# Layer 0's attention: its other products four at a time behind one of four steps, and gelus in threes

## The chip, the cores and the metric

The kernel runs on one core of a Trainium2 chip. Its time is the device time of one execution in microseconds; the median of three runs is given. The engines are TensorE (matmuls, with its weight loads apart), VectorE, ScalarE, GpSimd and SyncE, which issues most DMAs. A profile of one execution records when each instruction ran.

## The reference, cut to what matters

Four layers work on eight images of 384 channels and 32 x 32 pixels. The change lies in layer 0, and in it in the attention part:

```python
q = _dwproj(x, dw_q, g_q, b_q, pw_q).reshape(B, heads, hd, N)   # depthwise conv, batch norm, exact gelu, then pw
k = _dwproj(x, dw_k, g_k, b_k, pw_k).reshape(B, heads, hd, N)
v = _dwproj(x, dw_v, g_v, b_v, pw_v).reshape(B, heads, hd, N)
attn = jax.nn.softmax(jnp.einsum('bhcn,bhcm->bhnm', q, k) * scale, axis=-1)
out = jnp.einsum('bhnm,bhcm->bhcn', attn, v).reshape(B, C, H, W)
out = jnp.einsum('oc,bchw->bohw', w_out, out)
return _bn(out, g_out, b_out)
```

There are B = 8 images, 8 heads of 48 channels and N = 1024 pixels. Everything is in float32. The batch norm after the attention needs the moments of all images.

## The kernel before, in words

Layer 0 first runs the depthwise convolutions of all images and stores them (`raw`). Then comes the attention, which is the stretch from about 415 to 1845 us of the profile. An image's three tensors are loaded as `g` (`load_b`), and each gets its batch norm and gelu in place, in three chunks of 128 x 1024 (`gelu_chunk`, L483, on ScalarE). The gelus of image b + 1 are done during image b, at steps that the table `GELUS` names.

The heads are handled in four pairs. Three pairs hold the first channels of two heads each, the fourth is gathered by small DMAs (`gather_last`, L460) from the rows left over. An image has 32 **steps**: four pairs, times two halves of the query pixels (`h`), times four steps of two key blocks of 128 (`kc` = 0, 2, 4, 6; NS = 2). I number an image's steps 0 to 31. Four steps of one pair and half make a unit. The loop over steps does this:

- It issues the scores of the **next** step (`scores`, L623): eight matmuls a step, each in a tile of 64 rows by 64 columns of the array with 512 columns streamed, into two PSUM buffers `s` of two banks each. (The profile records each of the kernel's float32 matmuls as two, so a step's scores show as x16 and a product as x6.) ScalarE takes their exponential (L630), which gives `p`.
- If `GELUS` names this step, the gelus of the next image's chunks stand here on ScalarE, behind those exponentials.
- It weighs the values with this step's `p` (`weigh`, L638): again eight matmuls of 64 x 64 tiles, into two PSUM banks `pav` that are held for the whole unit.
- In some steps it takes other products from a queue, `todo`, and issues them. At the end of a unit VectorE normalises (`normalise`, L595 to L609): it reads the two `pav` banks, transposes, takes the reciprocal and writes `att`. For the fourth pair `place_last` (L471) copies the rows into `att` by twelve DMAs.

The other products use the whole 128 x 128 array. Each is one PSUM bank from the pool `bank` of four, which `pav` shares:

- `project` (L558): 3 matmuls by 512 columns give half of q or of k for one pair. The copy out alternates between ScalarE (first half) and VectorE (second half), through `evac` (L76, L78). After the second half, two small gathers go to SyncE's queue.
- `values` (L531): 3 matmuls by 384 columns give a block of 128 pixels of v, copied by VectorE (L538).
- `out_project` (L575): 3 matmuls by 512 columns of the output projection. It loads a piece `xh` of x (L572) and stores its result `ot` (L588), both by SyncE's queue, with two buffers each; VectorE copies, takes moments and forms two sums (L584, L587, L477, L478). In the last image ScalarE does the copy and issues the store.

An image queues, in this order: 4 projections at step 0, 6 output products of the image before at step 4, 4 projections at step 8, 8 values of the next image at step 16, and 4 projections of the next image at step 24. The first image's own values are also in the queue at the start, and the last image queues 3 of its own output products at step 28. ScalarE's order is the order of the program (`manual_schedule`); the other engines' orders are made by the framework's scheduler, which keeps each product group where the loop puts it on TensorE.

Of the kernel before, what the change touches and what calls it, by code (L numbers as in the profile page):

```python
# [15 lines left out]
KC = C // P  # L16
# [36 lines left out]
def tile_kernel(ctx: ExitStack, tc: tile.TileContext, i: dict, out: bass.AP):  # L53
# [10 lines left out]
    def big(name):  # L64
        return ps_big.tile([P, N], F32, tag="big", name=name)

    def bank(name):
        return ps_mm.tile([P, HALF], F32, tag="mm", name=name)
# [144 lines left out]
    def load_b(b):  # L213
        acts[b] = {}
        for v in (0, 1, 2) if b == 0 else (2, 1, 0):
            acts[b][v] = image(f"g{v}_{b}")
            load_image(acts[b][v], raw[v][b])

    with ExitStack() as pa:
# [120 lines left out]
        sts, taps, todo, later, normed = {}, [], {}, list(work), {0}  # L340
# [141 lines left out]
    def gelu_chunk(g, v, c):  # L482
        nc.scalar.activation(  # L483
            g[:, c, :], g[:, c, :], AF.Gelu,
            bias=ss0[:, v, 1, c : c + 1], scale=ss0[:, v, 0, c : c + 1],
        )
# [5 lines left out]
    with ExitStack() as pb:  # L492
# [10 lines left out]
        def values_tile(s):  # L503
            t = wb.tile([P, NT8, 2 * NH0, 32], F32, name=f"vt{s}")
            nc.gpsimd.memset(t, 0.0)
            nc.gpsimd.memset(t[:, :, :, HQ0 : HQ0 + 1], 1.0)
            vts.append(t)

        values_tile(0)
        for v, nm in enumerate(("wq0", "wk0", "wv0")):  # L510
# [9 lines left out]

        GELUS = {
            s: [divmod(i, KC) for i in range(2 * k, min(2 * k + 2, 3 * KC))]
            for k, s in enumerate((7, 9, 11, 13, 17))
        }

        def values(b, t):
            pv = bank(f"pv{b}_{t}")
            for c in range(KC):  # L530
                nc.tensor.matmul(  # L531
                    pv[:, :C],
                    lhsT=acts[b][2][:, c, t * P : (t + 1) * P],
                    rhs=w_in[2][:, c, :],
                    start=(c == 0),
                    stop=(c == KC - 1),
                )
            nc.vector.tensor_copy(  # L538
                vts[b % 2][:, t, :, :HQ0],
                pv[:, :C].rearrange("p (h d) -> p h d", d=HQ0),  # L540
            )

        def fetch(k):

            b, t = divmod(k, 2)
            fetched[b, t] = image(f"f{b}_{t}")
            load_image(fetched[b, t], o_dram[b] if t else x_img[b])

        def project(b, pr, v, h):
            if h == 0:  # L550
                qks[b, pr, v] = qp.tile([P, N], F32, tag=f"qk{v}", name=f"qk{v}_{b}_{pr}")
                if pr == 0:
                    qks[b, KC, v] = qp.tile(
                        [P, N], F32, tag=f"ql{v}", name=f"ql{v}_{b}", bufs=1
                    )
            pq = bank(f"pq{v}_{b}_{pr}_{h}")
            for c in range(KC):
                nc.tensor.matmul(  # L558
                    pq,
                    lhsT=w_in[v][:, c, pr * P : (pr + 1) * P],  # L560
                    rhs=acts[b][v][:, c, h * HALF : (h + 1) * HALF],
                    start=(c == 0),
                    stop=(c == KC - 1),
                )
            evac(qks[b, pr, v][:, h * HALF : (h + 1) * HALF], pq)
            if h == 1:
                gather_last(qks[b, KC, v], qks[b, pr, v], pr)

        def out_project(b, m, h):
            hs = slice(h * HALF, (h + 1) * HALF)  # L570
            xh = op.tile([P, HALF], F32, tag="xh", name=f"xh{b}_{m}_{h}")
            nc.sync.dma_start(out=xh, in_=x_img[b][:, m, hs])  # L572
            po = bank(f"po{b}_{m}_{h}")
            for c in range(KC):
                nc.tensor.matmul(  # L575
                    po,
                    lhsT=wo0[:, c, m * P : (m + 1) * P],
                    rhs=atts[b][:, c, hs],
                    start=(c == 0),
                    stop=(c == KC - 1),  # L580
                )
            ot = op.tile([P, HALF], F32, tag="ot", name=f"ot{b}_{m}_{h}")
            if b + 1 < B:
                nc.vector.tensor_copy(ot, po)  # L584
            else:
                nc.scalar.copy(ot, po)
            nc.vector.bn_stats(ost[:, m, 2 * b + h, :], ot)  # L587
            (nc.sync if b + 1 < B else nc.scalar).dma_start(out=o_dram[b, :, m, hs], in_=ot)  # L588
            cross(b, m, h, xh, ot)
# [43 lines left out]
        def weigh(b, pr, kc, pav, p):  # L633
            for k in range(2):
                r = slice(64 * k, 64 * k + 64)
                for j in range(2):
                    hd = 2 * pr + j
                    nc.tensor.matmul(  # L638
                        pav[k][64 * j : 64 * j + 64, :],
                        lhsT=vts[b % 2][r, kc, 2 * hd : 2 * hd + 2, :].rearrange(  # L640
                            "p a b -> p (a b)"
                        ),
                        rhs=p[r, j * HALF : (j + 1) * HALF],
                        start=(kc == 0),
                        stop=(kc == NT8 - 1),
                    )
# [8 lines left out]
        NS = 2  # L655
# [5 lines left out]
        todo = [lambda t=t: values(0, t) for t in range(NT8)]  # L661
        todo.pop(0)()

        def scores_of(b, pr, h, kc):
            return [scores(b, pr, h, kc + k) for k in range(NS)]
# [4 lines left out]
        for n, (b, pr, h, kc) in enumerate(steps):  # L670
            if kc == 0:
                if pr == 0 and h == 0:
                    atts[b] = ap_.tile([P, KC, N], F32, tag="att", name=f"att{b}")
                    if b + 1 < B:
                        load_b(b + 1)
                    else:
                        for k in range(3):
                            fetch(k)
                if b == 0 and pr == 1 and h == 0:
                    values_tile(1)  # L680
                if b + 1 == B and pr == 2 and h == 0:
                    for k in range(3, 5):
                        fetch(k)
                if b + 1 == B and pr == 3 and h == 1:
                    todo += [lambda m=m: out_project(B - 1, m, 0) for m in range(KC)]
                if h == 0 and pr + 1 < KC:
                    todo += [
                        lambda v=v, q=q, b=b, pr=pr: project(b, pr + 1, v, q)
                        for v in (1, 0) for q in range(2)
                    ]  # L690
                if pr == 0 and h == 1 and b > 0:
                    todo += [
                        lambda m=m, q=q, b=b: out_project(b - 1, m, q)
                        for m in range(KC) for q in range(2)
                    ]
                if pr == 2 and h == 0 and b + 1 < B:
                    todo += [lambda t=t, b=b: values(b + 1, t) for t in range(NT8)]
                if pr == 3 and h == 0 and b + 1 < B:
                    todo += [
                        lambda v=v, q=q, b=b: project(b + 1, 0, v, q)  # L700
                        for v in (1, 0) for q in range(2)
                    ]
                pav = [bank(f"pav{b}_{pr}_{h}_{k}") for k in range(2)]
            cur = nxt
            if n + 1 < len(steps):
                nxt = scores_of(*steps[n + 1])
            if b + 1 < B:
                for v, c in GELUS.get(n % (len(steps) // B), ()):
                    gelu_chunk(acts[b + 1][2 - v], 2 - v, c)
            for k in range(NS):  # L710
                weigh(b, pr, kc + k, pav, cur[k])

            if n % NS or (b == 0 and pr == 0 and h == 0):
                for _ in range(min(2, len(todo))):
                    todo.pop(0)()
            if kc == NT8 - NS:
                normalise(b, pr, h, pav)
# [19 lines left out]
    _, sco, sho = sc_o  # L737
# [51 lines left out]
    with tc.If(redo > 0):  # L789
        with ExitStack() as pb:  # L790
# [13 lines left out]
            with tc.For_i(0, B) as bi:  # L804
# [40 lines left out]
                for pr in range(NPAIR0):  # L845
                    qt, kt = qks[0][:, pr, :], qks[1][:, pr, :]
                    for h in range(2):
                        pav = bank(f"pav_e{pr}_{h}")
                        for j, r in enumerate(HR):
                            hd = 2 * pr + j  # L850
                            pt = qp.tile([P, NT8, HALF], F32, tag="pt", name=f"pt_e{pr}_{h}_{j}")
                            for qc in range(4):
                                q0 = h * HALF + qc * P
                                nm = f"_e{pr}_{h}_{j}_{qc}"
                                s = big(f"s{nm}")
# [13 lines left out]
                                for kg in range(2):  # L869
                                    tp = bank(f"tp{nm}_{kg}").rearrange("p (k q) -> p k q", k=4)  # L870
                                    for k in range(4):
                                        kc = kg * 4 + k
# [952 lines left out]
```

## Time and profile before

| what | value |
| --- | --- |
| three runs, us | 3834.8, 3829.8, 3833.54; median 3833.54 |
| the profiled execution's own time, us | 3834.06 |
| its span, first to last instruction, us | 3832.2 |
| mean granted TensorE clock | 0.975 |
| TensorE busy over the span, us | 3646.2 (95%) |
| period of one image of attention (first gelu to first gelu, images 3 and 4), us | 1179.34 - 1001.95 = 177.39 |
| exponentials of layer 0 (L630), us | 512 of 1.02 |
| gelus from L483 | 72 of 1.23 |
| loads of the gelu table (L483) and of the exponential's (L630) | 36 and 36, 1.28 each |

A line of a timeline gives the start in us from the span's start, the length in us, the engine, the line of the kernel, the operation, what it writes and reads, how many neighbouring instructions are merged into the line, and in brackets how long the engine stood idle ahead of it and who released it. PE is TensorE, PEld its weight loads, DVE VectorE, ACT ScalarE, POOL GpSimd, SP SyncE. Matmul ends are modelled, so distances between starts say more than lengths.

### The profile page before, as it was taken

To read this page: it belongs to the slowest core of one execution; us is meant where nothing else is said; L and a number is where in the kernel's file an instruction comes from. 1 tells how busy PE (TensorE), PEld (TensorE's weight loads), DVE (VectorE), ACT (ScalarE), POOL (GpSimd) and SP (SyncE) were. 2 spreads that over 40 slices of the span, in tenths; PEclk is the share of its full clock that TensorE was granted. 3 is DMA by queue.
4 is the path that set the end of the run, shared out by engine and by line. 5 is a ranking of instruction groups with operands and counts; after the bars stand their busy time and mean duration, and the time that the engine had idled before them with its cause. 6 is when DMAs were issued, how large, how long until landed. Compare 5 with 4: busy or idle time off the path is not lost.

```text
span 3832.2 us, 39353 instructions
## 1 busy us (share of the span) xinstructions
PE 3646.2 (95%) x15754; PEld 1520.9 (40%) x15754; DVE 1823.4 (48%) x2826; ACT 1314.7 (34%) x1557; POOL 235.5 (6%) x170
## 2 busy tenths in 40 slices
PE   7999899999999999999899999999999999999748
PEld 3444333333333333333344445444444444445213
DVE  5876223232323232332256665475656646565544
ACT  2222454554546353534112323223232222313102
POOL 0000000000000000000000100101011010100321
PEclk9999999999999999999899999999999999999868
DMA  6777211121202121111620000101001010010000
GB/s 200 245 235 241 100 53 43 53 61 40 74 24 72 27 69 38 59 49 50 233 81 33 17 33 19 48 17 33 33 17 34 17 50 17 25 42 1 17 17 18
DMA packets 83097, 242.64 MB, mean 63 GB/s; under 512 B 18336, under 2 KB 18864, under 8 KB 82520
## 3 DMA queue, kind: packets, MB, share of 16 engines
q1 hardware_dynamic: 69894, 200.56, 15.7%
q10 hardware_dynamic: 13008, 39.43, 3.0%
q8 instruction: 128, 2.10, 0.2%
q14 instruction: 67, 0.55, 0.0%
HBM read 122.78 MB, written 75.50 MB: 52 GB/s over the span
## 4 chain that ended last, share of the span: by engine, by line
PE 39%; DVE 9%; POOL 1%; issue 1%; ACT 1%; DVEq 0%; ACTq 0%; POOLq 0%
PE y L1251 10%; PE ph L1232 8%; DVE y L1320 5%; PE pq L1367 3%; PE pw L1341 3%; PE s L1504 3%; PE pf L1609 3%; PE pav L1520 2%; PE pss L1546 1%; DVE hd L1218 1%; DVE off L1415 1%; PE pk L1478 1%; PE xsb L1464 1%; PE pv L1487 1%; POOL tap L1323 1%
## 5 line engine op out<-in xcount | busy, mean ns | idle before, releaser
L630 ACT ACTIVATE p<-s 128x1024 f32<-128x1024 f32 x512 | 496.4, 1021 | 497.1 <-PE s L623 496.8
L1251 PE MATMUL y<-hd,w_sb 128*128 128x512 f32 x1080 | 493.4, 601 | 3.6 <-DVE hd L1218 3.6
L638 PE MATMUL pav<-p,vt 64*64 64x512 f32 x4096 | 486.4, 589 | 0.0
L1232 PE MATMUL ph<-h,w_sb 128*128 128x512 f32 x1104 | 483.6, 594 | 0.0
L623 PE MATMUL s<-qk,qk 48*64 48x512 f32 x3072 | 373.1, 600 | 4.4 <-ACT p L630 4.4
L381 PE MATMUL pk<-st,cw_sb 126*126 126x512 f32 x720 | 321.5, 608 | 3.6 <-DVE ga_a L118 3.3
L1232 PEld LDWEIGHTS ph<-h,w_sb 128*128 128x128 f32 x1104 | 207.8, 190 | 252.5 <-issue 249.4
L1251 PEld LDWEIGHTS y<-hd,w_sb 128*128 128x128 f32 x1080 | 198.8, 191 | 250.4 <-issue 236.3
L638 PEld LDWEIGHTS pav<-p,vt 64*64 64x64 f32 x4096 | 156.2, 133 | 285.3 <-issue 285.0
L595 DVE COPY ta<-pav 128x512 f32<-128x512 f32 x64 | 44.3, 692 | 439.1 <-PE pav L638 436.1
L1320 DVE SCALAR_TENSOR_TENSOR y<-h,tap,y 128x961 f32<-128x961 f32 (+1 forms) x184 | 233.5, 1295 | 1.6
L381 PEld LDWEIGHTS pk<-st,cw_sb 126*126 126x126 f32 x720 | 140.1, 197 | 177.7 <-issue 170.7
L1415 DVE SCALAR_TENSOR_TENSOR off<-q,dw_sb,off 128x225 f32<-128x225 f32 (+3 forms) x432 | 209.6, 542 | 1.9
L1240 ACT ACTIVATE hd<-ph,b_sb 128x512 f32<-128x512 f32 x180 | 122.6, 681 | 254.3 <-PE ph L1232 253.9
L623 PEld LDWEIGHTS s<-qk,qk 48*64 48x64 f32 x3072 | 102.6, 133 | 241.6 <-issue 184.7
L1341 PE MATMUL pw<-y,upw 128*128 128x512 f32 x288 | 128.6, 602 | 54.8 <-POOL y L1324 50.1
L78 DVE COPY qk<-pq 128x512 f32<-128x512 f32 x48 | 33.2, 692 | 293.1 <-PE pq L558 281.4
L387 ACT COPY y<-pk 126x512 f32<-126x512 f32 (+1 forms) x136 | 76.2, 583 | 254.4 <-DMA raw<-y 115.9
L1511 ACT ACTIVATE p<-s 128x1024 f32<-128x1024 f32 x96 | 93.0, 1021 | 171.8 <-PE s L1504 171.7
L146 ACT ACTIVATE h<-x,ss_d 128x1024 f32<-128x1024 f32 x42 | 49.6, 1231 | 287.6 <-DVE ss_d L132 287.6
L575 PE MATMUL po<-att,wo_sb 128*128 128x512 f32 x288 | 134.5, 617 | 9.5 <-DMA att<-al 9.5
L1218 DVE TENSOR_TENSOR hd<-hd,cb 128x512 f32<-128x512 f32 x180 | 122.9, 688 | 34.6 <-ACT hd L1240 34.2
(281 smaller groups left out, 4124.0 us busy)
## 6 DMA issues: line engine op xcount, KB each, us to landing
g<-raw SPq DMA_DIRECT2D x72, 512.0 KB
st<-pad SPq DMA_DIRECT2D x180, 168.0 KB
raw<-y ACTq DMA_DIRECT2D x180, 168.0 KB
xa<-in_x_dram SPq DMA_DIRECT2D x24, 512.0 KB
xh<-in_x_dram SPq DMA_DIRECT2D x48, 256.0 KB
f<-in_x_dram SPq DMA_DIRECT2D x24, 512.0 KB
f<-o SPq DMA_DIRECT2D x24, 512.0 KB
o<-ot SPq DMA_DIRECT2D x42, 256.0 KB
```

The source lines that it names most:

```text
L381: nc.tensor.matmul(pk[h].rearrange("p (h w) -> p h w", w=W)[: 3 * nch, :, o0 : o0 + c1 - c0], lhsT=lhs, rhs=rhs, start=(k == 0), stop=(k = ...
L575: nc.tensor.matmul(po, lhsT=wo0[:, c, m * P : (m + 1) * P], rhs=atts[b][:, c, hs], start=(c == 0), stop=(c == KC - 1),)
L623: nc.tensor.matmul(s[64 * k : 64 * k + 64, j * HALF : (j + 1) * HALF], lhsT=kt[r, k0 : k0 + 64], rhs=qt[r, h * HALF : (h + 1) * HALF], sta ...
L630: nc.scalar.activation(p, s, AF.Exp, scale=scale)
L638: nc.tensor.matmul(pav[k][64 * j : 64 * j + 64, :], lhsT=vts[b % 2][r, kc, 2 * hd : 2 * hd + 2, :].rearrange("p a b -> p (a b)"), rhs=p[r, ...
L1218: nc.vector.tensor_tensor(hd, hd, state["cb"], ALU.mult)
L1232: nc.tensor.matmul(ph, lhsT=w1[:, e, c, dc * P : (dc + 1) * P], rhs=state["h1"][c], start=(c == 0), stop=(c == KC - 1),)
L1240: nc.scalar.activation(hd, ph, AF.Relu, bias=b1[:, k : k + 1])
L1251: nc.tensor.matmul(y, lhsT=w2[:, e, dc, m * P : (m + 1) * P], rhs=state[h, k], start=(k == 0), stop=(k == NE * KC - 1),)
L1320: eng.scalar_tensor_tensor(d, f, tap2[:, c, t : t + 1], d, ALU.mult, ALU.add)
L1341: nc.tensor.matmul(pw[:, hs], lhsT=upw2[:, c, m * P : (m + 1) * P], rhs=y[:, c, hs], start=(c == 0), stop=(c == KC - 1),)
L1415: nc.vector.scalar_tensor_tensor(d, f, dw3[:, t : t + 1], d, ALU.mult, ALU.add)
```

## The change

Before, a step took up to two products from the queue when its number is odd (`n % NS`), which is two of the four steps of a unit, and in each of the first unit's four steps. Now the first unit stays as it was, and every other unit takes up to four products behind its second step (`kc == NS`, so steps 1, 5, 9, 13, ... of an image) and none behind its fourth.

The gelus of the next image stood two and two at steps 7, 9, 11 and 13 and one at step 17. Now they stand three and three at steps 9 (the tensor of v), 13 (k) and 17 (q). The number of products, of gelus and of DMAs is the same.

```diff
-        GELUS = {
-            s: [divmod(i, KC) for i in range(2 * k, min(2 * k + 2, 3 * KC))]
-            for k, s in enumerate((7, 9, 11, 13, 17))
-        }
+        GELUS = {s: [(v, c) for c in range(KC)] for v, s in enumerate((9, 13, 17))}
...
-            if n % NS or (b == 0 and pr == 0 and h == 0):
-                for _ in range(min(2, len(todo))):
+            early = b == 0 and pr == 0 and h == 0
+            if early or kc == NS:
+                for _ in range(min(2 if early else 4, len(todo))):
                     todo.pop(0)()
```

## The prediction

> **What bounds the kernel now.** I read the page's busy shares first, then the windows over layer 0's attention, image by image, then TensorE's timeline inside one image.
>
> Busy time of each engine, from the page:
>
> ```profile
> PE 3646.2 (95%) x15754; PEld 1520.9 (40%) x15754; DVE 1823.4 (48%) x2826; ACT 1314.7 (34%) x1557; POOL 235.5 (6%) x170
> ```
>
> One of the windows (PE, PEld, DVE, ACT, POOL busy, granted clock, DMA share, GB/s):
>
> ```profile
> 947.00:1125.00 178.00, 178.00 (x1192) 65.58 (x1188) 54.08 (x89) 89.47 (x90) 0.00 (x0) 1.00 0.17 52
> ```
>
> This is image 3's attention: TensorE busy all 178.00 us at a granted clock of 1.00, VectorE 54, ScalarE 89. TensorE is the bound, so a gain has to be time between its matmuls. "Busy" hides such time; the starts in the timeline (start, length, engine, line) show it:
>
> ```profile
> 1464.54 1.95 PE L623 MATMUL s<-ql,ql 48*64 48x512 f32 x16
> 1466.31 1.90 PE L638 MATMUL pav<-p,vt 64*64 64x512 f32 x16
> 1468.03 1.90 PE L623 MATMUL s<-ql,ql 48*64 48x512 f32 x16
> 1469.74 1.90 PE L638 MATMUL pav<-p,vt 64*64 64x512 f32 x16
> 1471.57 5.42 PE L558 MATMUL pq<-g,wq_sb 128*128 128x512 f32 x12
> 1476.92 1.95 PE L623 MATMUL s<-ql,ql 48*64 48x512 f32 x16
> ...
> ```
>
> A step is one s group and one pav group. Without products it takes 3.438 us (s starts at 1758.20 and, 14 steps on, at 1806.33): 8 rounds of four matmuls side by side, 0.4297 each. Two steps with one pair of projections take 1476.92 - 1464.54 = 12.38. Of that 2 x 3.438 = 6.876 are the steps and 12 x 0.4297 = 5.157 the products; 0.35 is left. For a pair of value products (128x384, so 12 x 0.322 = 3.87) the starts 1429.95 and 1441.06 leave 11.11 - 6.876 - 3.87 = 0.36. It lies at the two ends of the pair, not between its products, as the timeline of weight loads shows:
>
> ```profile
> 836.58 0.15 PEld L638 LDWEIGHTS pav<-p,vt 64*64 64x64 f32 x4 [0.28 <-issue]
> ...
> 837.54 0.30 PEld L575 LDWEIGHTS po<-att,wo_sb 128*128 128x128 f32 x2 [0.81 <-issue]
> ...
> 839.37 0.19 PEld L575 LDWEIGHTS po<-att,wo_sb 128*128 128x128 f32 x1 [0.24 <-issue]
> 839.79 0.19 PEld L575 LDWEIGHTS po<-att,wo_sb 128*128 128x128 f32 x1 [0.24 <-issue]
> ```
>
> The loads before and inside the group are 0.43 apart; 837.54 comes 0.96 after 836.58. The second product's first load (839.79) comes 0.42 after the sixth: a second product behind a first costs no switch. I price a group of products at **0.355 us**, whatever its length.
>
> [...] s and pav run as 64-row, 64-column tiles, the products on the full array, so each group is two changes; [...]the trace gives 0.355 for both. [...] the trace has 1.28 per load, 36 to gelu and 36 back to exp[...]. [...] Here a gap of 2.13 us (3.01 between weight loads, at 480.80 below) was followed by some 3 us of rounds 0.86 apart, and a like one (2.07, at 516.81) by none.
>
> **Part 1: pairs become fours.** Counting what the queue of products holds: image 0 had 13 groups (steps 0,1,2,3,5,9,11,17,19,21,23,25,27) and gets 9 (0,1,2,3,5,9,17,21,25): 4 fewer. Images 1 to 6 had 13 (1,3,...,13 and 17,...,27) and get 7 (1,5,9,13,17,21,25): 36 fewer. Image 7 had 9 and gets 5 (1,5,9,13,29): 3 fewer that count (3,7,11); step 31 is treated below. In all 43 x 0.355 = **-15.3**.
>
> Does a four stall? pav holds two of the four PSUM banks of its pool, so the third and fourth product take the banks of the first and second. In pairs of today the first product's copy starts 2.88 after the pair's start (837.54, copy 840.42) and takes 0.69, so its bank is free at 3.57; the third product wants it at 6 x 0.43 x 2 = 5.16. The second's copy (843.13) ends at 6.28; the fourth wants it at 7.73. Values: the first copy would end at 1.93 + 0.3 + 0.56 = 2.8 against 3.87. No wait: 0. Only image 0's step 9 is close: ScalarE's copy of the first product stands behind three gelus. With exps ending 3.15 after the step's s start, load 1.28, three gelus 3.72 and copy 0.58 it ends at 8.73; the third product wants it at 3.65 + 5.16 = 8.81. I take 0.2[...], bounds 0 and 1.
>
> What moves with the products: the output products issue an x load and a store each on SP, with two buffers each. Behind a fourth product VectorE may wait for a store or load; between its copies lie 2.6 us and it owes TensorE nothing until the next bank two steps later: 0. The small gathers of q and k rows are issued with their projections, and SP's later g loads queue behind them; those are for the image after the next and have over 150 us of slack: 0. GpSimd has nothing here.
>
> **Part 2: gelus in threes.** Two steps with a pair and a gelu group take 12.57 (s at 1375.36, then 1387.93) against 12.38: **0.19** a group, because the load back to exp starts only when the next s is there and delays two exps. A third gelu (1.235) does not lengthen this: in a pair ScalarE ends gelus and copy 8.73 after the step's s start, and the next s calls at about 10.2, a margin of 1.4 (in a four 6.6). Images 1 to 6 go from 5 groups to 3: 12 x 0.19 = **-2.3**.
>
> Image 0 differs, because two of its gelu groups stand in steps without products (timeline of TensorE, steps 10 and 15's s):
>
> ```profile
> 480.80 2.99 PE L623 MATMUL s<-qk,qk 48*64 48x512 f32 x16 [2.13 <-ACT p L630]
> ...
> 516.81 2.00 PE L623 MATMUL s<-qk,qk 48*64 48x512 f32 x16 [2.07 <-ACT p L630]
> ```
>
> They cost 2.4 each (s came 5.74 and 5.69 after the last, not 3.44, and the next step is 0.1 late), the other three 0.19: 5.4. After, step 7 is gone, steps 9 and 17 have fours (0.19 each, and the 0.2 above), but step 13 has no products, since all four stand at 9: three gelus there cost 2.4 + 1.24 = 3.6. Sum 4.2: **-1.2**. The half clock behind 480.80 cost 1.6 more; a gap of 3.3 at step 13 can call it as well, so I leave it as it is: bounds -1.6 and +1.6.
>
> **Part 3: the end of image 7.** Its last three products (output of the first half) stood two at step 29 and one at 31 (timeline of TensorE):
>
> ```profile
> 1821.72 1.95 PE L623 MATMUL s<-ql,ql 48*64 48x512 f32 x16
> 1823.49 3.62 PE L638 MATMUL pav<-p,vt 64*64 64x512 f32 x32
> 1827.03 2.84 PE L575 MATMUL po<-att,wo_sb 128*128 128x512 f32 x6
> 1834.83 10.56 PE L575 MATMUL po<-att,wo_sb 128*128 128x512 f32 x18 [4.96 <-DMA att<-al]
> ```
>
> The one at 1827.03 runs while VectorE normalises the last pav and DMAs bring it to att, until 1834.83: it is free today. At step 29 it stands ahead of the last pav groups and pushes that chain back by 6 x 0.43 = **+2.6**; its cover is gone. Bounds: 0.6 less, if ScalarE's queue, then free of this product's copy and store, starts its att DMAs sooner; 1.3 more at half clock (a stretch at half clock lies near 1816).
>
> **Sum.** -15.3 - 2.3 - 1.2 + 2.6 = -16.2. The profiled execution took 3834.06 (span 3832.2 and 1.86 around it), 0.5 above the median of the runs, 3833.54. So 3834.06 - 16.2 = 3817.9 on its scale, and **3817.4** on the median's. What follows layer 0 doesn't change.
>
> **Rivals.**
> (a) *The 0.35 belongs to products, not groups* (for instance to the first use of a bank). Then 43 changes save nothing: -2.3 - 1.2 + 2.6 = -0.9, 3832.6, no change. Against: the even 0.42 to 0.43 inside the pair. 6%.
> (b) *Bank waits take the place of the switches; slower.* If the third product finds its bank only when the second's copy is done, it waits 6.28 - 5.16 = 1.1 in the 29 fours of 512 columns and about 0.85 in the 14 of values: 31.9 + 11.9 = 43.8, net +27.6, 3861. It decides from 16.2 / 43 = 0.38 a four. For: two free banks for four products. Against: in the built program the third projection waits for ScalarE's count and the fourth for VectorE's, so each for its own bank, and copies have 1.1 to 1.6 us to spare. 4%.
> (c) *A little more*: image 0's half clock goes (-1.6) and the end costs 0.6 less, with switches of 0.37 (-0.6): 3814.6. 14%.
> (d) *A little less*: two fours per image wait 0.4 for a copy behind gelus or x loads (13 x 0.4 = 5.2): 3822.6. 16%.
> The forecast itself has 60%.
>
> **How the numbers follow.** About 0.2% (7.7 us) can be told from no change. Forecast, (c) and (d) are faster: 90%; (a) is the same: 6%; (b) slower: 4%. Runs of before spread over 5 us, so each case is taken with 2 us around it: 3812.5 (under c) to 3825 (over d) leaves out (a) and (b).
>
> **What would show it.** In the timeline of after: product groups of 24 matmuls about 10.7 us long, s starts 17.5 apart around a four and a step (6.88 + 10.31 + 0.35), the image period down from 177.4 to about 174.9 us; 22 loads of gelu tables in place of 36 in this stage; one stall of about 3.3 on ScalarE in image 0; the last pav group directly followed by the wait for att. A wait of matmuls on ScalarE's or VectorE's copies inside the fours would prove (b) or (d), and a period of about 177.0 (a).

## The result, and the profile after

The changed kernel takes 3814.64 us (median; 3811.21 to 3817.26) against 3832.85 us before in the same comparison: ratio 0.9953, 95% interval 0.9935 to 0.997. That is 18.2 us less, clear of no change; 3817.4 had been forecast, 16.2 less than the 3833.54 of the three runs known then. The profiled execution of after has a span of 3811.5 us.

The page's first part, busy time of each engine:

```profile
PE 3620.1 (95%) x15754; PEld 1526.5 (40%) x15754; DVE 1828.2 (48%) x2826; ACT 1278.1 (34%) x1529; POOL 235.5 (6%) x170
```

TensorE has the same 15754 matmuls and the same share. ScalarE lost 28 instructions (1557 to 1529), the 14 gelu groups' loads there and back, and 36.6 us of busy time. That ScalarE's time is not where the gain lies is seen only in the experiments.

A window of the same length as that of before, in the middle of the stage (PE, PEld, DVE, ACT, POOL busy, granted clock, DMA share, GB/s):

```profile
945.00:1123.00 178.00, 178.00 (x1212) 67.79 (x1208) 54.82 (x90) 85.59 (x87) 0.00 (x0) 1.00 0.17 52
```

TensorE is as busy as before, but 1212 matmuls start in 178 us where 1192 did: the busy share could not show this gain, the counts do (roughly, for the two windows don't begin at the same step).

TensorE's timeline around one four, the projections behind step 1 of an image:

```profile
1126.08 1.90 PE L620 MATMUL s<-qk,qk 48*64 48x512 f32 x16
1127.80 1.90 PE L635 MATMUL pav<-p,vt 64*64 64x512 f32 x16
1129.62 5.42 PE L555 MATMUL pq<-g,wk_sb 128*128 128x512 f32 x12
1134.88 5.31 PE L555 MATMUL pq<-g,wq_sb 128*128 128x512 f32 x12
1140.12 1.95 PE L620 MATMUL s<-qk,qk 48*64 48x512 f32 x16
1141.89 1.90 PE L635 MATMUL pav<-p,vt 64*64 64x512 f32 x16
1143.61 1.90 PE L620 MATMUL s<-qk,qk 48*64 48x512 f32 x16
```

From s to the second s behind it are 1143.61 - 1126.08 = 17.53 us; 17.5 had been forecast. The two pairs merge without a gap, as the weight loads at the seam and the four's end show:

```profile
1134.02 0.19 PEld L555 LDWEIGHTS pq<-g,wk_sb 128*128 128x128 f32 x1 [0.24 <-issue]
1134.45 0.19 PEld L555 LDWEIGHTS pq<-g,wq_sb 128*128 128x128 f32 x1 [0.24 <-issue]
1134.88 0.19 PEld L555 LDWEIGHTS pq<-g,wq_sb 128*128 128x128 f32 x1 [0.24 <-issue]
...
1139.17 0.19 PEld L555 LDWEIGHTS pq<-g,wq_sb 128*128 128x128 f32 x1 [0.24 <-issue]
1140.12 0.21 PEld L620 LDWEIGHTS s<-qk,qk 48*64 48x64 f32 x8 [0.76 <-issue]
```

Loads stand 0.43 apart across the seam (1134.45, 1134.88), and 0.95 at the change back to the small tiles (1140.12). That is a distance of loads, and not all of them stand the same time ahead of their matmuls: the one at 1134.45 stands 0.43 ahead (its matmul starts at 1134.88), the one at 1140.12 not at all. By the starts of matmuls, TensorE's own loss for both changes of this four is 17.53 - 6.88 - 10.31 = 0.34. Between 520 and 1780 us the list of waits has no line for TensorE's matmuls at all: no four waits for a copy out.

For comparing kernels I use the **stage**: from the first s group of the attention to the first gate matmul (plog) of layer 1. It takes 1860.13 - 419.81 = 1440.32 us before and 1840.75 - 417.17 = 1423.58 after, **-16.7**. The rest of the profiled difference (20.7 in the spans) is 2.6 ahead of the stage and 1.3 behind it, where both kernels run the same code. The start of the stage lay between 412.7 and 422.1 us in the eleven profiled kernels, so a difference of some us between two single executions needs this split.

### The profile page after: what moved, and what is told of

Its sections match the earlier page's. It is cut to its first block, busy times and chain, and to the rows that moved or that the text cites. A ratio compares the mean times of both kernels' runs of the same rounds, so it can differ in the third digit from the quotient of the medians.

```text
span 3811.5 us, 39331 instructions
## 1 busy us (share of the span) xinstructions
PE 3620.1 (95%) x15754; PEld 1526.5 (40%) x15754; DVE 1828.2 (48%) x2826; ACT 1278.1 (34%) x1529; POOL 235.5 (6%) x170
## 4 chain that ended last, share of the span: by engine, by line
PE 39%; DVE 9%; POOL 1%; issue 1%; ACT 1%; DVEq 0%; ACTq 0%; POOLq 0%
PE y L1249 11%; PE ph L1230 8%; DVE y L1318 5%; PE pq L1365 3%; PE s L1502 3%; PE pw L1339 3%; PE pf L1607 3%; PE pav L1518 2%; PE pss L1544 1%; DVE hd L1216 1%; DVE off L1413 1%; PE pk L1476 1%; PE xsb L1462 1%; PE pv L1485 1%; POOL tap L1321 1%
```

## The experiments

Theory T is that of the prediction: a group of full-array products costs 0.355 us, whatever its length; a gelu group 0.19 beside products and over 2 in a step without; and the last image's third product lost its cover, 2.6. Rivals: A, the 0.35 belongs to each product, and the fewer table loads brought the gain; B, the end is set by DMAs, not by TensorE; C, long groups wait for the copies out. All nine kernels were timed beside the kernel before; differences are of medians, each to its own kernel before (3832.57 for the first four, 3832.24 for the next four, 3833.58 for the last). The period is that of an image in the middle of the stage, from an image's first gelu to the next image's.

| kernel | us | ratio to before, 95% interval | difference | stage | period |
| --- | --- | --- | --- | --- | --- |
| before | 3832.85 | | | 1440.32 | 177.39 |
| after | 3814.64 | 0.9953 (0.9935 to 0.997) | -18.2 | 1423.58 | 174.87 |
| fours only | 3856.06 | 1.0064 (1.005 to 1.0077) | +23.5 | 1466.47 | 179.64 to 184.60 |
| gelus only | 3827.82 | 0.999 (0.9983 to 0.9996) | -4.8 | 1438.25 | 177.02 |
| fours, five gelu groups | 3813.19 | 0.9958 (0.9945 to 0.9971) | -19.4 | 1424.05 | 175.30 |
| split fours | 3830.2 | 0.9994 (0.9987 to 1.0) | -2.4 | 1439.66 | 177.01 |
| last two and one | 3809.62 | 0.9942 (0.9929 to 0.9956) | -22.6 | 1419.53 | 174.87 |
| last three at the end | 3802.61 | 0.9918 (0.9905 to 0.9932) | -29.6 | 1410.64 | 174.88 |
| gelus at 9, 17, 21 | 3809.24 | 0.9943 (0.993 to 0.9957) | -23.0 | 1419.76 | 174.92 |
| eights | 3799.45 | 0.9921 (0.9907 to 0.9934) | -32.8 | 1411.15 | 174.17 |
| eights and the end | 3790.66 | 0.9889 (0.9872 to 0.9905) | -42.9 | 1400.61 | 174.17 |

### One part alone: fours only, and gelus only

Fours only is the changed kernel with the old table of gelus:

```diff
-        GELUS = {s: [(v, c) for c in range(KC)] for v, s in enumerate((9, 13, 17))}
+        GELUS = {
+            s: [divmod(i, KC) for i in range(2 * k, min(2 * k + 2, 3 * KC))]
+            for k, s in enumerate((7, 9, 11, 13, 17))
+        }
```

> The fours of the change with the gelus where they stood before (two each behind steps 7, 9, 11, 13 and one behind 17). Theory T (a group of products costs 0.355 us[...], a gelu group 0.19 beside products and 2.4 in a step without): fours -15.3, end of image 7 +2.6, but steps 7 and 11 now have no products in images 1 to 6, so 12 gelu groups go from 0.19 to 2.4: +26.5, and image 0 gets one bare group more: +2.2. Net +16 against before, about 3849, and up to 20 more where a gap calls the half clock. Rival A (0.35 belongs to each product, the change gained by fewer table loads): +31, about 3864. In the trace T wants product groups of 24 matmuls with no more lost time than pairs, and two stalls of about 2.1 on ScalarE per image.

Measured: 23.5 slower than before, within what T allowed, but midway between T's 16 and A's 31; the periods decide. TensorE's timeline, image 3 (two of its bare steps):

```profile
1015.06 3.34 PE L623 MATMUL s<-qk,qk 48*64 48x512 f32 x16 [2.13 <-ACT p L630]
...
1020.35 5.42 PE L575 MATMUL po<-att,wo_sb 128*128 128x512 f32 x12
1025.60 5.31 PE L558 MATMUL pq<-g,wk_sb 128*128 128x512 f32 x12
...
1043.65 2.00 PE L623 MATMUL s<-qk,qk 48*64 48x512 f32 x16 [2.07 <-ACT p L630]
```

The fours cost what they should (the second pair starts 5.25 behind the first), but the gelus behind steps 7 and 11 now have nothing beside them, and TensorE stands 2.13 and 2.07 us. The shortest period, 179.64, is 4.3 over that of the same fours with gelus beside products (175.30, below): 2.2 more for each of two bare groups, as T had it. A, under which the fours save nothing, would put the period at 177.39 + 4.4 = 181.8 at least. The other periods are 181.28 or more, because TensorE ran at half clock for a while: behind the gap ahead of 1015.06 the s group took 3.34, and the granted clock was 0.56 from there to 1018.30 (1.00 from 1043.65 to 1047.10, behind the other gap). In images 2 to 5 these stretches add 9.9, which with T's 16 comes near the 26.2 by which the stage is longer. So each half of the change needs the other: the gelus had to move to where the products went.

Gelus only is the kernel before with the new table:

> The gelus in threes behind steps 9, 13, 17, the products in pairs as before. Theory T: 12 gelu groups fewer beside products, -2.3; image 0 loses its bare group at step 7 and has three gelus at the bare step 13: -1.2 (half clock of 1.6 either way). Net -3.5 against before, about 3829.4. Rival A (the gain comes from 14 pairs of table loads less, 36 us of ScalarE): nearly the whole gain of the change, -18, about 3815.

Measured: 4.8 less by the medians and 2.1 less in the stage (T: 3.5), period 177.02 (T: 177.01). With 22 table loads of gelus in place of 36, most of the change's 18.2 (16.7 in the stage) is missing. Rival A's source of the gain falls here.

### Fours with five gelu groups

```diff
-        GELUS = {s: [(v, c) for c in range(KC)] for v, s in enumerate((9, 13, 17))}
+        GELUS = {5: [(0, 0)], 9: [(0, 1), (0, 2)], 13: [(1, 0), (1, 1)], 17: [(1, 2), (2, 0)],
+                 21: [(2, 1), (2, 2)]}
```

> Fours as in the change, but five gelu groups an image as before, each behind a step with products: one behind 5, two behind each of 9, 13, 17, 21. Theory T: fours -15.3, end +2.6, no saving on groups of gelus in images 1 to 6, image 0 with one bare group of two at step 13 in place of two: -2.2. Net -14.9 against before, about 3818; image period 177.39 - 6 x 0.355 = 175.3. Rival A (the number of table loads decides): no gain, 3833 or a little above.

Measured: 19.4 less (T: 14.9), period 175.30 as T said. With all 36 loads in place, fours bring the gain, as long as the gelus stand beside products. (177.39 - 175.30) / 6 = 0.348 per group saved. Its median is 1.4 under that of the change, less than the runs spread; by the stage it is 0.5 longer. T has it 1.3 longer (-14.9 against -16.2), without the half clock: behind its gap of 2.12 in image 0 none followed (the s group took 2.00), while the change lost some 1.7 to it there (shown further below).

### Split fours

The same kernel as the change, but each four is put half ahead of the weighing and half behind it, in the same step:

```diff
+            early = b == 0 and pr == 0 and h == 0
+            split = not early and kc == NS and len(todo) > 3
+            if split:
+                for _ in range(2):
+                    todo.pop(0)()
             for k in range(NS):
                 weigh(b, pr, kc + k, pav, cur[k])
...
-            early = b == 0 and pr == 0 and h == 0
             if early or kc == NS:
-                for _ in range(min(2 if early else 4, len(todo))):
+                for _ in range(min(2 if early or kc == NS and split else 4, len(todo))):
```

> The changed kernel with each four split within its step: two products between scores and weighing, two behind the weighing. Products, table loads, evictions and steps are the same; only 43 more groups. Theory T: 43 x 0.355 = +15.3 against the changed kernel, about 3830, image period 174.87 + 2.1 = 177.0. Rival A (0.35 belongs to each product): no difference, 3814.6.

Measured: 3830.2, 15.8 of the change's gain given back (-2.4 against -18.2), period 177.01. Its timeline has the pav group between two pairs:

```profile
1136.57 5.42 PE L555 MATMUL pq<-g,wk_sb 128*128 128x512 f32 x12
1141.92 1.95 PE L635 MATMUL pav<-p,vt 64*64 64x512 f32 x16
1143.80 5.42 PE L555 MATMUL pq<-g,wq_sb 128*128 128x512 f32 x12
```

(177.01 - 174.87) / 6 = 0.357 per group added. Products, steps, loads of tables and copies are those of the change; only 43 groups are new. This is the test of the price of a group, and rival A (no difference) is out. What it shows is the price of a group that stands between small-tile groups, 0.357 us for its two changes of tile shape. What in the two changes costs it, no run here shows.

### The end of the last image

Last two and one takes the last image's own three products as the kernel before did:

```diff
             early = b == 0 and pr == 0 and h == 0
-            if early or kc == NS:
-                for _ in range(min(2 if early else 4, len(todo))):
+            tail = b + 1 == B and pr == 3 and h == 1
+            if early or kc == NS or (tail and n % NS):
+                for _ in range(min(2 if early or tail else 4, len(todo))):
```

> The changed kernel with the last image's three own output products taken as before, two behind step 29 and one behind step 31. Theory T (moving the third product from step 31 to 29 took away its cover, 6 x 0.43 = 2.6): -2.6 against the changed kernel, about 3812. Rival B (the end is set by the DMAs to att, not by TensorE): no difference, 3814.6.

Measured: 22.6 less than before, 4.4 better than the change. From the table load ahead of the gelus in image 6 to the gate matmuls it takes 310.64 against 313.00, -2.4, near T's -2.6. The other 1.7 in the stage is chance: the same code in image 0 (from the first s to the table load ahead of image 1's first gelu) took 234.53 against 236.22, because the gap of 3.25 us there was not followed by half clock this time (the s and pav groups behind it took 2.00 and 1.90, in the change 2.19 and 3.47).

Slow stretches at the end touch both kernels (here two matmuls at 1789.78 took 2.04 where the two at 1787.09 took 1.10; in the change the 14 at 1794.75 ran at a granted clock of 0.73), so the 2.4 is a sum of several things. The wait itself shows the cover more plainly. This kernel's end, on TensorE:

```profile
1797.61 1.95 PE L620 MATMUL s<-ql,ql 48*64 48x512 f32 x16
1799.38 3.62 PE L635 MATMUL pav<-p,vt 64*64 64x512 f32 x32
1802.92 2.84 PE L572 MATMUL po<-att,wo_sb 128*128 128x512 f32 x6
1810.73 10.61 PE L572 MATMUL po<-att,wo_sb 128*128 128x512 f32 x18 [4.97 <-DMA att<-al]
```

From the last s to the last three products are 1810.73 - 1797.61 = 13.12 with a product in between, and 1816.38 - 1803.17 = 13.21 in the change without one (lines below): there the product was free.

Last three at the end puts them behind the last step, with VectorE copying:

```diff
-            if b + 1 < B:
+            if b + 1 < B or h == 0:
                 nc.vector.tensor_copy(ot, po)
...
-            if early or kc == NS:
+            tail = b + 1 == B and pr == 3 and h == 1
+            if not tail and (early or kc == NS):
...
                 normalise(b, pr, h, pav)
+                if tail:
+                    while todo:
+                        todo.pop(0)()
```

> The changed kernel with all three of these products behind the last step, after its normalisation in the program, VectorE copying them out. Theory T: they run while VectorE and the DMAs bring the last rows to att, so their 7.7 leave the path, and the wait of 3.95 for the first half's rows at step 29 mostly goes too; VectorE's sums for six products in a row give some 2 back. About -9 to -12 against the changed kernel, 3803 to 3806. Rival B: at most -2.

Measured: 29.6 less than before, 11.4 better than the change, within T's 9 to 12. In the stage it is 12.9; of that, 2.2 is half clock that the change's 14 matmuls at 1794.75 met. TensorE's timeline, first of the change, then of this kernel:

```profile
1789.39 1.10 PE L572 MATMUL po<-att,wo_sb 128*128 128x512 f32 x2 [1.38 <-DMA att<-al]
1792.07 1.69 PE L572 MATMUL po<-att,wo_sb 128*128 128x512 f32 x2 [1.58 <-DMA att<-al]
1794.75 8.49 PE L572 MATMUL po<-att,wo_sb 128*128 128x512 f32 x14 [0.99 <-DMA att<-al]
1803.17 1.95 PE L620 MATMUL s<-ql,ql 48*64 48x512 f32 x16
1804.94 3.62 PE L635 MATMUL pav<-p,vt 64*64 64x512 f32 x32
1816.38 9.63 PE L572 MATMUL po<-att,wo_sb 128*128 128x512 f32 x18 [7.83 <-DMA att<-al]
```

```profile
1794.54 3.61 PE L635 MATMUL pav<-p,vt 64*64 64x512 f32 x32
1798.09 8.99 PE L572 MATMUL po<-att,wo_sb 128*128 128x512 f32 x20
1807.49 7.11 PE L572 MATMUL po<-att,wo_sb 128*128 128x512 f32 x16 [0.42 <-DMA att<-al]
```

In the change three waits for the first half's rows and one of 7.83 for the second's stand in the path. Here the last pav comes first, the three products cover the wait for the second half's rows, and 0.42 is left. Behind it the small batch norm begins later on VectorE, as said: its mean matmul waits 8.73 instead of 5.32. Rival B (at most -2) is out.

### Gelus behind 9, 17 and 21

```diff
-        GELUS = {s: [(v, c) for c in range(KC)] for v, s in enumerate((9, 13, 17))}
+        GELUS = {s: [(v, c) for c in range(KC)] for v, s in enumerate((9, 17, 21))}
```

> The changed kernel with the gelus in threes behind steps 9, 17 and 21, which all have fours, in every image. Theory T: image 0's bare group at step 13 goes: -3.4, and -1.7 of half clock behind it; images 1 to 6 unchanged (a group costs 0.19 beside two products or four). About -5, 3809.5, image period 174.87 as in the changed kernel. Rival A: the period falls, because a pair did not hide three gelus.

Measured: 23.0 less than before, 4.8 better than the change. From the first s to the table load ahead of image 1's first gelu it takes 231.61 against 236.22, -4.6 (T: -5.1), and the period is 174.92: a pair had hidden three gelus as well as a four does. The other reading, under which the period falls, is out.

### Eights, and both together

```diff
-        GELUS = {s: [(v, c) for c in range(KC)] for v, s in enumerate((9, 13, 17))}
+        GELUS = {s: [(v, c) for c in range(KC)] for v, s in enumerate((5, 9, 17))}
...
-                for _ in range(min(2 if early else 4, len(todo))):
+                for _ in range(min(2 if early else 8, len(todo))):
```

> The changed kernel with up to eight products behind the second step of a unit (so 4, 6, 4, 8, 4 an image behind steps 1, 5, 9, 17, 25) and gelus in threes behind 5, 9 and 17. Theory T: 14 groups fewer, 14 x 0.355 = -5.0; image 0 has products behind all three gelu groups, -3.4 - 1.7. About -10, 3804.5, image period 174.87 - 0.71 = 174.16. Rival C (with two free banks, long groups wait for the copies out: VectorE needs 2.85 for an output product, TensorE 2.58): a wait of up to 2 in each group of six and a period of 175 or more.

Measured: 14.6 better than the change, more than forecast; period 174.17, as T said, where C wanted 175 or more. Groups of six and eight show no wait of matmuls in the list of waits either, so C is out for these lengths. In the stage it is 12.4: the 10.1 of T, and 2.3 because the 14 matmuls at the end, 8.49 in the change (shown above), took 6.25 here; their granted clock was 1.00 here and 0.73 there. The other 2 of the medians no single profile can place.

Eights and the end joins this with the last three at the end.

> Both best parts together: up to eight products a group with gelus in threes behind steps 5, 9, 17, and the last image's three own products behind its last step. The two touch different places, so theory T adds what each gave against the changed kernel: -15.2 and -12.0, so about 3787.5. Were the gains of run and of place not separate (for instance because both came from the same half-clock stretches), at least 5 less.

Measured: 3790.66, ratio 0.9889, the fastest version, but 3.2 slower than forecast. In the stage it gains 23.0 over the change, where the two parts had 12.4 and 12.9. That is 2.4 less than their sum, near the 2.2 of the change's half clock at 1794.75, which both parts had counted and which can be saved only once.

## Why the prediction was right, point by point

- **A group of products costs 0.355.** Measured 0.348 (saved, five gelu groups) and 0.357 (added, split fours). The count of 43 groups and the 15.3 stand: split fours gave back 15.8.
- **Fours don't wait for banks.** Right; no such wait in the trace. At image 0's step 9, where I had guessed 0.2, it was close: ScalarE's copy ended at 484.24 and the third product's first weight load followed at 484.30, 0.50 behind the load before it instead of 0.43. Its matmuls lost nothing: they start 5.25 behind the first product's (479.40, 484.65), as in other fours. The three gelus took 3.50 in a row, not the 3.72 that I had summed from single ones.
- **0.19 a gelu group beside products.** 0.37 per image for two groups in gelus only, 0.43 between five groups and three: 0.19 to 0.22.
- **Image 0's bare step.** TensorE's timeline of after:

```profile
503.88 1.90 PE L620 MATMUL s<-qk,qk 48*64 48x512 f32 x16
505.60 1.90 PE L635 MATMUL pav<-p,vt 64*64 64x512 f32 x16
510.76 2.19 PE L620 MATMUL s<-qk,qk 48*64 48x512 f32 x16 [3.25 <-ACT p L627]
512.70 3.47 PE L635 MATMUL pav<-p,vt 64*64 64x512 f32 x16
515.99 1.90 PE L620 MATMUL s<-qk,qk 48*64 48x512 f32 x16
```

  Here s comes 6.88 after the last instead of 3.44, 3.4 lost (3.6 said; the third gelu adds 1.13, not 1.24, for two in a row had taken 2.37), and the pav group of 3.47 shows the half clock that I had left as it was: the granted clock was 0.57 from 512 to 516 us.
- **The end costs 2.6.** 2.4 by last two and one. The bound of 0.6 less was not used.
- **Sum.** -16.7 in the stage for -16.2. By image, between first exponentials: -2.8 in image 0 (-2.6 said), -15.4 in images 1 to 6 (-15.1), and +1.5 from image 7's first exponential to the gate matmuls (+1.5). In the last there is luck: before and after both met half clock at the end (granted clock 0.71 from 1816.67 to 1821.70 before, 0.73 at 1794.75 after). By an estimate from the 6.18 that 14 of these matmuls took to the next s in eights, and 0.43 for each, it cost some 1.5 before (8 matmuls, 5.05) and 2.2 after (14, 8.42). The median's 18.2 differs by 1.5 more, no more than the executions' spread; that part was not traced to a cause.

Of the rivals, (a) falls by split fours and gelus only, (b) by the list of waits. (d) falls with it. The median lies on (c)'s 3814.6, but the profiles don't show what (c) said: image 0's half clock was there, the end cost 2.4 and not 2.0, and a group 0.348 to 0.357, not 0.37.

## What to carry to other kernels

Where TensorE is the bound and always "busy", look at the distances between starts around each change of tile shape, and count the changes: here each group of products cost 0.348 to 0.357 us, and more products of one shape in a group added nothing to that, up to eight in a row, as copies kept up with two free banks (no wait of matmuls for them, period 174.17). Work of two engines that runs side by side must move together: the gelus that hid behind products stalled TensorE by 2.07 and 2.13 us once the products had gone. Ask of every product near a serial end whether it covers a wait; here that brought twice as much (11.4) as the next best of what was tried on top of the change (the bare step of image 0, 4.8, or fewer groups, 5.0 by T).

## What the runs showed of the hardware that was not expected

The prediction had seen one gap of 2.13 us followed by half clock; how often short gaps are followed by it, and that the same code meets it in one execution and not in another, was not expected. Of 15 gaps of 1.96 to 2.13 us in fours only, 6 were followed by slow s groups (2.97 to 3.69 us instead of 2.00). Of five profiled kernels with the gap of 3.25 or 3.26 us in image 0's step 13 (the change, gelus only, split fours, last two and one, last three at the end), four met half clock behind it. What sets a gap with half clock behind it apart from one without, no run here shows. Most of these stretches cost 1.6 to 1.7 us. The longest, behind the gap ahead of 1196.35 in fours only, has a granted clock of 0.51 from 1196.35 to 1203.30 and cost 3.3; with a second one it makes image 4's period of 184.60.
